# First weights and samples asked for by counts and the eight largest of one row; the first pair as a plain product

## The chip, the cores and the metric

The kernel runs on one core of a Trainium2 chip. The metric is device time in microseconds (us), from runs of the whole program; beside them stands one profiled execution, from which every view of the profile comes.

## What is computed

There are 128 samples of 128 tokens with 1024 features, and an integer role (one of three) for each sample. Two layers follow each other, and in both the sample's role picks the weights, the biases and the vectors of the normalisation:

```python
h = jnp.einsum('bsh,bhk->bsk', hidden_states, W_down[role]) + b_down[role][:, None, :]   # 1024 -> 512
h = jax.nn.gelu(h, approximate=False)
u = jnp.einsum('bsk,bkh->bsh', h, W_up[role]) + b_up[role][:, None, :]                   # 512 -> 1024
y = hidden_states + u
mean = jnp.mean(y, axis=-1, keepdims=True)
var = jnp.mean(jnp.square(y - mean), axis=-1, keepdims=True)
yn = (y - mean) * jax.lax.rsqrt(var + LN_EPS)
return yn * gamma[role][:, None, :] + beta[role][:, None, :]
```

All of it is in float32. The roles are known only on the chip.

## The kernel before, in words

**Order of the samples.** Because weights depend on the role, the kernel first sorts the samples by role, on the chip. The roles come in one DMA as a row of 128 integers (L249). VectorE cleans the row (L282 to L284), TensorE turns it into a column, comparisons and two matmuls count roles and ranks (L290 to L300), and a few dozen small VectorE operations give each sample its slot. The role with the most samples gets place 0, and so on. Three matmuls in `gathered` (L323 to L330) make three small integer rows: `perm` (which sample stands in slot n, L332), `role_of` (which role has place k, L343) and `place` (which place slot n has, L348). An engine that issues a DMA for "the sample of slot 0" or "the weights of place 0" first loads such a number into a register (`reg`, L351), so it waits for the row it reads. `counted` (L241) is a VectorE operation with a sum along the row; `zeros` (L264) issues matmuls of 128x512 zeros whose results nobody reads; nine of them stand behind the sort (L349).

**Pairs.** Two samples of one role make a pair (256 tokens). There are 63 such pairs and one last item for samples left over. Four phases follow each other (down and up of the first layer, down and up of the second), and each goes over all items. In a down phase a pair is multiplied with a 1024x512 weight by a seven-product scheme of the Strassen-Winograd kind (`item_products`, L431): the two samples are the two halves of the rows, the features and the columns are halved too, and seven products of 128x256 blocks, with four steps over the features each, take the place of eight. For this the weights must be given as blocks and differences of blocks (B11, B21, B22, T1, T2, T3, T4; for the first phase `first_sum`, L159, makes the T blocks out of the raw rows), and three sums of the pair's own blocks are needed (`winograd_sums`, L396). The bias gets in by a copy of the bias table into the accumulator bank ahead of the products (`seeded`, L424), where the right half of the table holds right minus left (`subtract`).

**A down item.** `load` and `load_rest` fetch the two samples in four quarters each, by SP's queue (`quartered`, L382). `turn` (L526) transposes a sample in 32x32 blocks on VectorE; `prepare` (L536) turns both samples and makes the sums (on GpSimd, for the first pair on VectorE), and for the first pair it makes T1 as well. Then the seven products follow, and the results go through a Gelu on ScalarE into the tensor `hd` in memory.

**Order of the work.** Every step is put on a heap with a time in units of a product slot (seven to a pair, 1.727 us each) and taken off in order of time (`at`, L734, and the loop at the end). On each engine the instructions are chained in that order, DMA requests on the queues of SP and ACT included. So each queue is strictly in order, and an instruction that waits holds up all that is behind it on its own engine. The first pair has times of its own (L474), with the product of T1 second.

**First weights.** The raw rows of place 0 (1024x512, 2 MB) are fetched in two blocks of 1 MB, `rows_of[0]` and `rows_of[1]`. `load_rows` (L145) makes four requests for a block, one for each quarter of the partitions, and the block's requests are split over the queues of ACT and SP; the second ACT half of block 1 stands behind the first two seeds on ACT. All of them read `role_of`, and the samples' requests read `perm`.

Of the kernel before, what the change touches and what calls it, by code (L numbers as in the profile page):

```python
# [26 lines left out]
def kernel(  # L27
# [117 lines left out]
    def load_rows(k, place, engine, kind, quadrants=range(NQ)):  # L145
        w = layers[0][0]
        role = reg(role_of, place, [kind], R - 1)
        for q in quadrants:
            src = w[ds(role, 1), ds(q * H // NQ, H // NQ), :]
            src = src.rearrange("o (i m) c -> i (o m) c", i=SQ)  # L150
            engine.dma_start(
                rows_of[k][ts(q, SQ), place].rearrange("p j h c -> p j (h c)"), src[:, ts(k, NQ)]
            )
# [87 lines left out]
    def counted(o, in0, scalar, op0, in1):  # L241

        n = in0.shape[1]
        nc.vector.scalar_tensor_tensor(
            junk[:, 0:n], in0, scalar, in1, op0, ALU.mult, accum_out=o
        )
# [22 lines left out]
    iota_row, iota_col, ones, upper = f32(B), f32(1), f32(B), f32(B)  # L269
    junk, wide = f32(B), f32(SQ)  # L270
    iota_r, ones_r = iota_row[:, 0:R], ones[:, 0:R]
    eps = const.tile([P, 1], F32, name="eps")
    nc.vector.memset(eps, LN_EPS)
    nc.vector.memset(ones, 1.0)
    nc.vector.tensor_copy(iota_row, iota_i)
    nc.vector.tensor_copy(iota_col, iota_c)
    nc.vector.tensor_scalar(upper, iota_row, iota_col, None, ALU.is_gt)
    nc.vector.tensor_copy(wide, iota_col.to_broadcast((P, SQ)))


    role_row = f32(B)[0:1]
    nc.vector.tensor_scalar(role_row, raw, float(-R), float(R - 1), ALU.max, ALU.min)  # L282
    nc.vector.tensor_scalar(junk[0:1], role_row, 0.0, float(R), ALU.is_lt, ALU.mult)
    nc.vector.tensor_tensor(role_row, role_row, junk[0:1], ALU.add)  # L284
# [4 lines left out]
    ps = bank_a("own_ps")  # L289
    nc.tensor.matmul(ps[:, 0:1], role_row, ones[0:1, 0:1], start=True, stop=True)  # L290
    role_col, is_own = f32(1), f32(R)
    nc.vector.tensor_copy(role_col, ps[:, 0:1])
    nc.vector.tensor_scalar(is_own, iota_r, role_col, None, ALU.is_equal)

    ps = bank_a("count_ps")
    nc.tensor.matmul(ps[:, 0:R], upper, is_own, start=True, stop=True)
    nc.tensor.matmul(ps[:, R : 2 * R], ones, is_own, start=True, stop=True)
    counts = f32(2 * R)
    nc.vector.tensor_copy(counts, ps[:, 0 : 2 * R])
    before, count = counts[:, 0:R], counts[:, R : 2 * R]  # L300

    key, odd, even = f32(R), f32(R), f32(R)
    nc.vector.scalar_tensor_tensor(key, count, float(R + 1), iota_r, ALU.mult, ALU.subtract)
    count_i = const.tile([P, R], I32, name="count_i")
    nc.vector.tensor_copy(count_i, count)
    nc.vector.tensor_scalar(count_i, count_i, 1, None, ALU.bitwise_and)
    nc.vector.tensor_copy(odd, count_i)
    nc.vector.tensor_tensor(even, count, odd, ALU.subtract)

    rank, own_key, base_, rest, own, slot, left, move = (f32(1) for _ in range(8))  # L310
    counted(own_key, is_own, 1.0, ALU.mult, key)
    counted(rank, is_own, 1.0, ALU.mult, before)
    counted(own, is_own, 1.0, ALU.mult, even)
    counted(base_, key, own_key, ALU.is_gt, even)
    counted(rest, key, own_key, ALU.is_gt, odd)
    nc.vector.tensor_tensor(slot, base_, rank, ALU.add)
    nc.vector.tensor_tensor(left, rank, own, ALU.is_ge)
# [3 lines left out]
    nc.vector.tensor_scalar(onehot, iota_row, slot, None, ALU.is_equal)  # L321

# [9 lines left out]
    perm = gathered("perm", wide, onehot)  # L332

# [9 lines left out]
    role_of = gathered("role_of", wide[0:R], at_place)  # L343

# [4 lines left out]
    zeros("bbbeeebbb")  # L349
# [32 lines left out]
    def quartered(t, srcs):  # L382

        for s, src in enumerate(srcs):
            n = src.shape[-1] // NQ
            for q in range(NQ):
                nc.sync.dma_start(
                    t[s][ts(q, SQ)], src[:, ts(q, n)].rearrange("(a t) c -> t a c", t=SQ)
                )
# [41 lines left out]
    def item_products(item, cols):  # L431
# [9 lines left out]
        if n < NPAIR:  # L441
            r = item.places[0]

            def s1():
                product(ps["b"], A(0, 0), w["B11"], r, cols)
                item.begin(0, 0, ps["b"])

            def s2():
                ps["a"] = bank("a", item.tag)
                product(ps["a"], A(0, 1), w["B21"], r, cols, True)  # L450
                item.end(0, 0, ps["a"])

            def s3():
                product(ps["b"], sums[:, 0], w["T2"], r, cols)
                item.begin(0, 1, ps["b"])

            def s4():
                product(ps["e"], A(1, 0), w["T1"], r, cols)
                item.begin(1, 1, ps["e"])

            def s5():
                product(ps["b"], sums[:, 1], w["T3"], r, cols)
                item.end(1, 1, ps["b"])

            def s6():
                product(ps["e"], sums[:, 2], w["B22"], r, cols)
                item.end(0, 1, ps["e"])

            def s7():
                product(ps["b"], A(1, 1), w["T4"], r, cols)  # L470
                item.whole(1, 0, ps["b"])


            times = (0, 2, 4, 1, 6.5, 6, 8) if item.early else range(0, 14, 2)  # L474
            steps = list(zip(times, (s1, s2, s3, s4, s5, s6, s7)))
            te = -3.9 if item.early else 1.5
            return steps + [(item.SEED, lambda: seed("b", "b", r)), (te, lambda: seed("e", "e", r))]
# [25 lines left out]
    class Down:  # L503
# [7 lines left out]
        def load(self):  # L511
            if self.among_weights:


                block = self.ph.weights[ORDER[self.m]].v
                self.xq = [block[:, 1 + s] for s in range(2)]
            else:
                self.xq = [flat("q", 4, f"xq{self.tag}_{s}", H) for s in range(2)]
            self.xq = [t.rearrange("p (a c) -> p a c", a=NQ) for t in self.xq]
            self.srcs = x_of(self.layer, self.n, ENG.SP)  # L520
            quartered(self.xq[0:1], self.srcs[0:1])

        def load_rest(self):
            quartered(self.xq[1:2], self.srcs[1:2])

        def turn(self, s):  # L526
            nc.vector.transpose(  # L527
                self.a[:, s].rearrange("p j (t a) -> p j a t", t=SQ),
                self.xq[s].rearrange("p a (i j) -> p j a i", i=SQ),
            )  # L530

        def begin_turns(self):
            self.a = flat("t", 3, "xT" + self.tag).rearrange("p (s j c) -> p s j c", s=2, c=P)
            self.turn(0)

        def prepare(self):  # L536
            if not self.among_weights:
                self.begin_turns()
            if self.early:
                first_sum("T1", 0)  # L540
            self.turn(1)
            self.sums = None
            if self.n < NPAIR:
                self.sums = flat("s", 3, "S" + self.tag, 1792)[:, 0:1536].rearrange(
                    "p (m j c) -> p m j c", m=3, c=P
                )
                winograd_sums(self.sums, self.a, nc.vector if self.early else nc.gpsimd)
            set_places(self, [ENG.PE, ENG.Activation])

        def products(self):  # L550
            return [(-0.5, self.first)] + item_products(self, K // 2)
# [191 lines left out]
    for k, ph in enumerate(phases):  # L743
        for m, n in enumerate(sequence):
# [17 lines left out]
            elif k == 0:  # L762
                first = {0: -30, 1: -19, 2: -19, 3: -17.4}.get(m, -19)
                rest = -27 if m == 0 else first + 0.05
            else:
                first = -15 if m == 0 else -11.9
                rest = first + 0.1
# [10 lines left out]
            prepare = {1: 3.5 - base, 2: 8.6 - base}.get(m, kind.PREPARE) if k == 0 else kind.PREPARE  # L778
# [4 lines left out]
        if k + 1 < len(phases):  # L783
# [17 lines left out]
            else:  # L801


                def first_bias(nxt=nxt):
                    nxt.bias = row = const.tile([P, 1, K], F32, name="first_bias")
# [45 lines left out]
    at(-29, lambda: load_bias([0], nc.scalar))  # L851
    at(-29, lambda: load_rows(0, 0, nc.scalar, ENG.Activation, (0, 1)))
    at(-28, lambda: load_rows(0, 0, nc.sync, ENG.SP, (2, 3)))
    at(-27, lambda: subtract(slice(0, 1)))
    at(-26, lambda: load_rows(1, 0, nc.sync, ENG.SP, (2, 3)))
    at(-3, lambda: load_rows(1, 0, nc.scalar, ENG.Activation, (0, 1)))
    for i, name in enumerate(("T2", "T3", "T4")):
        at(-2.5 + i / 10, lambda name=name: first_sum(name, 0))
    at(14.7, lambda: load_bias(range(1, R)))
    at(20.7, lambda: subtract(slice(1, R)))  # L860
    for k in range(1, R):
        start = SLOTS * 2 * k
        at(start + 4.25, lambda k=k: load_rows(0, k, nc.sync, ENG.SP))
        at(start + 8.25, lambda k=k: load_rows(1, k, nc.sync, ENG.SP))
# [44 lines left out]
```

## Time and profile before

| what | value |
|---|---|
| median of 3 runs | 3143.81 us (3142.12 to 3145.17) |
| profiled execution | 3143.59 us |
| its span, first to last instruction | 3141.8 us |
| TensorE busy | 3109.3 us, 99% of the span |
| VectorE, ScalarE, GpSimd busy | 1977.3, 1203.6, 1793.9 us |
| `perm` ready, `role_of` ready | 9.06, 10.45 us after the span's start |
| first matmul of the first pair | 20.85 us |
| first matmul of the second pair | 39.72 us |
| DMA over the span | 642.21 MB, 204 GB/s |

Times in the views are microseconds from the span's start. PE is TensorE, PEld its weight loads, DVE is VectorE, ACT ScalarE, POOL GpSimd, SP the engine that issues most DMAs; a "q" behind a name is the engine's queue of instructions that aren't counted as busy. A name such as `xTd<-xqd` says what is written and what is read; "[4.78 <-DVE xTd L402]" is idle time of the engine ahead of the instruction and what ended it. A float32 matmul is two instructions in the trace.

### The profile page before, as it was taken

The page shows a single profiled execution, that of the slowest core. Times are in us where ns is not written, and L with a number is a line of the kernel's source. Part 1 is how long each engine was busy: PE and PEld are TensorE (multiplying, and loading weights), DVE is VectorE, ACT ScalarE, POOL GpSimd, SP SyncE. Part 2 cuts the span into 40 slices and gives each one's busy share as a digit, 9 for nine tenths or more (in the row PEclk, how much of TensorE's full clock was granted, in tenths as well). Part 3 has the DMA queues.
Part 4 walks back from the last instruction along what each step waited for, and adds up shares of the span by engine and source line. Part 5 has one row for each costly group of instructions (what it writes and reads, how often), then busy time and mean ns, then how long its engine had stood idle before and what let it go on. Part 6 is the DMA issues. An engine that isn't in the chain of part 4 may idle for free.

```text
span 3141.8 us, 42319 instructions
## 1 busy us (share of the span) xinstructions
PE 3109.3 (99%) x10806; PEld 2053.3 (65%) x10806; DVE 1977.3 (63%) x2794; ACT 1203.6 (38%) x2814; POOL 1793.9 (57%) x1396
## 2 busy tenths in 40 slices
PE   8999999999999999999999999999999999999998
PEld 6888888888544444444478888888884444444443
DVE  5655445454578777788854444444447777787777
ACT  1222222222445455555432222222224545554554
POOL 3544444444577767777654443444436777677776
PEclk9999999999999999999999999999999999999999
DMA  8888878886786666666796555555568766666665
GB/s 191 207 209 213 209 206 210 212 213 191 278 286 222 218 217 218 217 223 216 235 260 164 128 135 128 134 125 137 126 184 292 264 219 216 218 217 221 215 226 175
DMA packets 430165, 642.21 MB, mean 204 GB/s; under 512 B 36081, under 2 KB 305906, under 8 KB 428786
## 3 DMA queue, kind: packets, MB, share of 16 engines
q1 hardware_dynamic: 429458, 637.94, 69.1%
q8 instruction: 102, 1.67, 0.2%
q10 hardware_dynamic: 480, 1.57, 0.2%
q14 instruction: 125, 1.02, 0.1%
HBM read 405.01 MB, written 234.36 MB: 204 GB/s over the span
## 4 chain that ended last, share of the span: by engine, by line
PE 48%; DMA 1%; DVE 1%; issue 0%; ACT 0%; DVEq 0%; SPq 0%; ACTq 0%
PE bu L410 14%; PE bd L410 14%; PE eu L410 7%; PE ed L410 7%; PE au L410 3%; PE ad L410 3%; DMA mid<-ou 0%; DVE ou L719 0%; DMA wall<-mid 0%; DMA hd<-hd 0%; ACT ou L704 0%; DVE xu L635 0%; DVE last_stat L636 0%; DVE xu L638 0%; DVEq L905 0%
## 5 line engine op out<-in xcount | busy, mean ns | idle before, releaser
L410 PE MATMUL bu<-wall,hTu 128*128 (+1 forms) x2048 | 922.0, 592 | 2.1 <-POOL ou L717 0.7
L527 DVE STREAM_TRANSPOSE xTd<-xqd 128x1024 f32<-128x1024 f32 x250 | 505.0, 2087 | 354.1 <-PE bd L410 275.4
L410 PEld LDWEIGHTS bu<-wall,hTu 128*128 128x128 f32 x2048 | 388.7, 190 | 490.9 <-issue 455.6
L401 POOL TENSOR_TENSOR Sd<-xTd 128x512 f32<-128x512 f32 x125 | 160.5, 1284 | 802.6 <-DVE xTd L527 798.7
L706 POOL TENSOR_TENSOR varu<-varu,mhalf 128x1 f32<-128x1 f32 x254 | 333.7, 1314 | 383.1 <-ACT varu L705 383.1
L410 PE MATMUL bd<-wall,xTd 128*128 (+1 forms) x2080 | 490.9, 379 | 1.4 <-DMA wall<-T 0.8
L410 PE MATMUL eu<-wall,hTu 128*128 (+1 forms) x1040 | 488.0, 592 | 0.0
L709 DVE SCALAR_TENSOR_TENSOR ou<-xu,meanu,tables 128x1024 f32<-128x1024 f32 x254 | 327.1, 1288 | 253.3 <-ACT ou L704 253.0
L410 PE MATMUL bd<-wall,Sd 128*128 (+1 forms) x2016 | 476.5, 379 | 2.3 <-ACT hd L560 1.6
L410 PEld LDWEIGHTS bd<-wall,xTd 128*128 128x128 f32 x2080 | 394.9, 190 | 58.0 <-issue 3.5
L410 PEld LDWEIGHTS bd<-wall,Sd 128*128 128x128 f32 x2016 | 382.8, 190 | 56.7 <-issue 4.1
L565 ACT ACTIVATE hd<-hd 128x256 f32<-128x256 f32 x382 | 159.4, 418 | 536.4 <-DVE hd L564 536.4
L410 PEld LDWEIGHTS eu<-wall,hTu 128*128 128x128 f32 x1040 | 197.6, 190 | 247.5 <-issue 229.6
L700 ACT ACTIVATE partu<-statu 128x2 f32<-128x2 f32 x254 | 51.9, 204 | 730.6 <-DVE xu L638 730.6
L717 POOL TENSOR_TENSOR ou<-ou,tables 128x1024 f32<-128x1024 f32 x127 | 299.5, 2358 | 0.1
L704 ACT ACTIVATE ou<-xu,meanu 128x1024 f32<-128x1024 f32 x254 | 292.2, 1150 | 8.3
L410 PE MATMUL ed<-wall,xTd 128*128 (+1 forms) x1072 | 254.6, 381 | 4.8 <-DVE xTd L402 4.8
L401 POOL TENSOR_TENSOR hTu<-hTu 128x256 f32<-128x256 f32 x126 | 205.3, 1630 | 66.3 <-DVE hTu L607 54.4
L410 PE MATMUL ed<-wall,Sd 128*128 (+1 forms) x1008 | 238.2, 379 | 0.1
L410 PE MATMUL ad<-wall,xTd 128*128 (+1 forms) x1008 | 238.2, 379 | 0.0
L410 PE MATMUL au<-wall,hTu 128*128 (+1 forms) x504 | 236.8, 592 | 0.0
L410 PEld LDWEIGHTS ed<-wall,xTd 128*128 128x128 f32 x1072 | 204.5, 191 | 33.6 <-issue 5.6
(114 smaller groups left out, 3349.8 us busy)
## 6 DMA issues: line engine op xcount, KB each, us to landing
xqd<-in_x_dram SPq DMA_DIRECT2D x512, 128.0 KB, 3.3
hd<-hd SPq DMA_DIRECT2D x256, 256.0 KB, 2.4
xu<-in_x_dram SPq DMA_DIRECT2D x128, 512.0 KB, 5.0
mid<-ou SPq DMA_DIRECT2D x128, 512.0 KB, 6.1
xu<-mid SPq DMA_DIRECT2D x128, 512.0 KB, 5.8
out_dram<-ou SPq DMA_DIRECT2D x126, 512.0 KB, 5.5
hqu<-hd SPq DMA_DIRECT2D x244, 256.0 KB, 6.5
xqd<-mid SPq DMA_DIRECT2D x488, 128.0 KB, 3.8
```

What stands on the lines that cost most here:

```text
L401: engine.tensor_tensor(dst[:, 1], a11, a21, ALU.subtract)
L410: nc.tensor.matmul(ps[:, 0:cols], a[:, j], w.rhs(r, j, cols), start=start and j == 0, stop=j == n - 1, skip_group_check=True,)
L527: nc.vector.transpose(self.a[:, s].rearrange("p j (t a) -> p j a t", t=SQ), self.xq[s].rearrange("p a (i j) -> p j a i", i=SQ),)
L565: nc.scalar.activation(y, y, AF.Gelu)
L700: nc.scalar.mul(part, self.stat[:, s], -1.0 / H)
L704: nc.scalar.activation(box["o"], self.x[:, s], AF.Square, bias=m, accum_out=v)
L706: nc.gpsimd.tensor_tensor(v, v, mhalf[:, 0:1], ALU.pow)
L709: nc.vector.scalar_tensor_tensor(box["o"], self.x[:, s], box["m"][:, 0:1], row(self.ph.gamma), ALU.add, ALU.mult)
L717: nc.gpsimd.tensor_tensor(o, o, row(self.ph.beta), ALU.add)
```

## The change

Five things are changed together.

1. The roles are counted on one row of one partition, by three `counted` operations; the role with the largest key comes out as an integer `role_0`, and the first samples of that role come out by the operation that gives the eight largest of a row (`first_two`, of which two are used). Both stand ahead of the sort. A matmul copies the row with roles, counts and keys to all partitions, and the sort goes on from there with three 128-wide counts. Zero matmuls are spread over the sort instead of standing behind it.
2. The first pair's samples, the weights' rows of place 0 and the first bias row are asked for by `role_0` and `first_two`. A block of rows is one request of 128 partitions (for all places). Block 0 is asked for on ACT, block 1 on SP; the first sample's quarters are split over SP and ACT.
3. The first pair doesn't use the seven products: `plain` multiplies each sample with the raw rows, in 512 columns, behind a one-row matmul that puts in the bias. Its samples are turned in halves. It makes no sums.
4. T1 to T4 of place 0 are made at new times; the bias table's first row is loaded later on ACT (-26 instead of -29), and its difference is taken at 0.3.
5. The second pair (m = 1) keeps the default order of products, its `prepare` goes from 3.5 to 4.5, and its sums are made on VectorE.

```diff
-    def load_rows(k, place, engine, kind, quadrants=range(NQ)):
-        w = layers[0][0]
-        role = reg(role_of, place, [kind], R - 1)
-        for q in quadrants:
-            src = w[ds(role, 1), ds(q * H // NQ, H // NQ), :]
-            src = src.rearrange("o (i m) c -> i (o m) c", i=SQ)
-            engine.dma_start(
-                rows_of[k][ts(q, SQ), place].rearrange("p j h c -> p j (h c)"), src[:, ts(k, NQ)]
-            )
+    def load_rows(k, place, queue):
+        role = reg(role_of, place, [queue.engine], R - 1) if place else reg(role_0, 0, [queue.engine], R - 1)
+        src = layers[0][0][ds(role, 1)].rearrange("o (p m) c -> p (o m) c", p=P)
+        queue.dma_start(rows_of[k][:, place].rearrange("p j h c -> p j (h c)"), src[:, ts(k, NQ)])
...
+    zeros("bb")
...
+    nc.vector.tensor_scalar(falling, iota_row[0:1], -1.0, float(B), ALU.mult, ALU.add)
+    nc.vector.tensor_scalar(same, iota_row, iota_col, None, ALU.is_equal)
+    nc.vector.tensor_scalar(earlier, iota_row, iota_col, None, ALU.is_lt)
+    row = f32(B + 2 * R)
+    role_1, count_1, key_1 = row[0:1, 0:B], row[0:1, B : B + R], row[0:1, B + R :]
...
+    for r in range(R):
+        counted(count_1[:, r : r + 1], role_1, float(r), ALU.is_equal, ones[0:1])
+    nc.vector.scalar_tensor_tensor(key_1, count_1, float(R + 1), iota_r[0:1], ALU.mult, ALU.subtract)
+    ps = bank_a("row_ps")
+    nc.tensor.matmul(ps[:, 0 : B + 2 * R], ones[0:1, 0:P], row[0:1], start=True, stop=True)
+    zeros("beee")
+    role_row, key = ps[:, 0:B], f32(R)
...
+    nc.vector.tensor_reduce(top, key_1, AX.X, ALU.max)
+    counted(role_f, key_1, top, ALU.is_equal, iota_r[0:1])
+    role_0 = const.tile([1, 1], I32, name="role_0")
+    nc.vector.tensor_copy(role_0, role_f)
+    nc.vector.scalar_tensor_tensor(junk[0:1], role_1, role_f, falling, ALU.is_equal, ALU.mult)
+    nc.vector.max(out=first_f, in_=junk[0:1])
+    first_two = const.tile([1, 8], I32, name="first_two")
+    nc.vector.tensor_scalar(first_two, first_f, -1.0, float(B), ALU.mult, ALU.add)
+    nc.vector.tensor_copy(counts[:, 0:R], ps[:, B : B + R])
+    nc.vector.tensor_copy(key, ps[:, B + R : B + 2 * R])
+    counted(role_col, role_row, 1.0, ALU.mult, same)
+    counted(rank, role_row, role_col, ALU.is_equal, earlier)
+    counted(counts[:, R:], role_row, role_col, ALU.is_equal, ones)
...
     perm = gathered("perm", wide, onehot)
+    zeros("bb")
...
     role_of = gathered("role_of", wide[0:R], at_place)
+    zeros("bb")
...
     place = gathered("place", wide_place, onehot)
-    zeros("bbbeeebbb")
+    zeros("bb")
...
+            if self.early:
+                for k, queue in enumerate((nc.sync, nc.scalar)):
+                    quartered(self.xq[0:1], [self.early_x(0, queue.engine)], (2 * k, 2 * k + 1), queue)
+                return
...
+    def plain(self):
+        self.ps = [None, None]
+        def half(s, k):
+            if k == 0:
+                self.ps[s] = bank("a", f"{self.tag}_{s}")
+                nc.tensor.matmul(self.ps[s], ones[0:1, 0:P], bias_row, start=True, stop=False)
+            for j in range(NQ):
+                rows = rows_of[k][:, 0, j].rearrange("p h c -> p (h c)")
+                nc.tensor.matmul(
+                    self.ps[s], self.a[:, s, NQ * k + j], rows, start=False, stop=k == 1 and j == NQ - 1
+                )
+            if k == 1:
+                nc.scalar.activation(self.h[s], self.ps[s], AF.Gelu)
+        steps = [(4 * s + 2 * k, lambda s=s, k=k: half(s, k)) for s in range(2) for k in range(2)]
+        return steps + [(0.1 + k / 10, lambda k=k: self.turn(1, ts(k, NQ))) for k in range(2)]
...
-            prepare = {1: 3.5 - base, 2: 8.6 - base}.get(m, kind.PREPARE) if k == 0 else kind.PREPARE
+            prepare = {1: 4.5 - base, 2: 8.6 - base}.get(m, kind.PREPARE) if k == 0 else kind.PREPARE
...
-    at(-29, lambda: load_bias([0], nc.scalar))
-    at(-29, lambda: load_rows(0, 0, nc.scalar, ENG.Activation, (0, 1)))
-    at(-28, lambda: load_rows(0, 0, nc.sync, ENG.SP, (2, 3)))
-    at(-27, lambda: subtract(slice(0, 1)))
-    at(-26, lambda: load_rows(1, 0, nc.sync, ENG.SP, (2, 3)))
-    at(-3, lambda: load_rows(1, 0, nc.scalar, ENG.Activation, (0, 1)))
-    for i, name in enumerate(("T2", "T3", "T4")):
-        at(-2.5 + i / 10, lambda name=name: first_sum(name, 0))
+    at(-31, lambda: load_rows(0, 0, nc.scalar))
+    at(-30.5, load_bias_row)
+    at(-29, lambda: load_rows(1, 0, nc.sync))
+    at(-26, lambda: load_bias([0], nc.scalar))
+    at(0.3, lambda: subtract(slice(0, 1)))
+    for t, name in zip((-8.7, -2.5, 4.6, 4.7), ("T1", "T2", "T3", "T4")):
+        at(t, lambda name=name: first_sum(name, 0))
```

The first bias row shares one small tile (`first_rows`) with the first bias of layer 1, which had a tile of its own. `load_bias_row` is a DMA of one row on ACT. The first sample is asked for at -30, the second at -28 (it was -27).

## The prediction

> **What bounds the kernel now.** I read the page first, then the busy time in stretches, then the start-up instruction by instruction, then the DMA queues. The page:
>
> ```profile
> span 3141.8 us, 42319 instructions
> PE 3109.3 (99%) x10806; PEld 2053.3 (65%) x10806; DVE 1977.3 (63%) x2794; ACT 1203.6 (38%) x2814; POOL 1793.9 (57%) x1396
> ```
>
> TensorE is busy all but 32.5 us. Stretches (length, then busy time of each engine, granted clock, DMA share, GB/s):
>
> ```profile
> 0.00:21.00 21.00, 12.43 (x31) 5.98 (x32) 9.56 (x48) 2.17 (x4) 1.10 (x7) 1.00 0.43 107
> 21.00:27.60 6.60, 1.82 (x9) 1.29 (x9) 4.36 (x5) 0.37 (x1) 0.00 (x0) 1.00 0.98 227
> 27.60:39.72 12.12, 12.12 (x48) 10.38 (x49) 11.23 (x10) 2.27 (x6) 4.28 (x3) 0.86 0.91 192
> 39.72:51.81 12.09, 12.09 (x58) 10.64 (x57) 7.74 (x6) 3.53 (x10) 11.54 (x10) 1.00 0.91 231
> ```
>
> The second pair starts at 39.72 and from there a pair costs 12.09 us without a gap (7 products of 1.727). So what matters is when TensorE may begin the second pair; after that everything follows it. The start-up, from the timeline (start, length, engine, line):
>
> ```profile
> 2.17 0.21 DVE L282 TENSOR_SCALAR sorting<-raw 1x128 f32<-1x128 int32 x1
> ...
> 8.78 0.28 DVE L329 CAST perm<-perm_ps 1x128 int32<-1x128 f32 x1 [0.73 <-PE perm_ps L327]
> ...
> 10.09 1.92 SPq L387 DMA_DIRECT2D xqd<-in_x_dram  x4
> 10.30 0.15 DVE L329 CAST role_of<-role_of_ps 1x3 int32<-1x3 f32 x1 [0.42 <-PE role_of_ps L327]
> ...
> 12.09 0.86 ACTq L151 DMA_DIRECT2D wall<-in_L_cond_W_down_dram  x2
> ...
> 20.85 1.97 PE L410 MATMUL bd<-wall,xTd 128*128 128x256 f32 x8
> ...
> 27.60 3.58 PE L410 MATMUL ed<-wall,xTd 128*128 128x256 f32 x8 [4.78 <-DVE xTd L402]
> ```
>
> Samples are asked for 7.9 us after the roles are read (2.17 to 10.09), weights 9.9 us after. One product runs at 20.85, then TensorE waits 4.78 us for the second sample and its sums, and restarts at a low clock. The transfers between 13 and 15 us, by queue (q1 is SP, q10 ACT; packets, MB, share):
>
> ```profile
> q10 hardware_dynamic: 135, 0.39, 82.4%
> q1 hardware_dynamic: 146, 0.15, 23.7%
> ```
>
> While both queues run, weights (ACT) take 195 GB/s and samples (SP) 73, together 266. One more line, from SP's own waits:
>
> ```profile
> SPq L151 <- DMA tables<-in_L_cond_b_down_dram: 2.6, 1, 2.6
> ```
>
> SP's second weight request, at 15.64, waits for the bias DMA, eight requests earlier: the waits fit eight completion semaphores used in turn.
>
> [...] weight loads of the zero matmuls stand 0.86 us apart at 12.50 and 13.36, and 0.43 from 14.18. [...]
>
> **The change, part by part.**
>
> *Count and first eight on one row.* Two mask rows more stand ahead of the roles (about 0.5 us), so the clean row of roles, done at 2.94 now, is done at 3.4. Three counts: a 3-wide count has a cadence of 0.21 to 0.27, and 128 elements cost 0.13 more (L277 0.29 against L303 0.16), so 0.35 each: 4.45. Key, largest, role and integer copy: 0.2 + 0.2 + 0.35 + 0.2. The role is ready at 5.4 instead of 10.45. First samples: 0.3 for the marked row, the largest-eight between 0.2 (nearest row) and 0.8, I take 0.35, and 0.2: 6.2 instead of 9.06. The tensor reduction isn't in the trace either: 0.15 to 0.4.
>
> *Requests.* From role to ACT's first request now: 10.45 to 11.15, 0.7; a further register load brings the next 0.94 later. So block 0 of weights is asked for at 6.1 on ACT, the bias row (2 KB) at 7.0, the sample quarters 2 and 3 at 8.0 and 8.5. SP, with two register loads as now (9.06 to 10.09): quarters 0 and 1 at 7.2 and 7.7, block 1 at 8.6, then sample 1. Its second quarter waits for block 0, eight requests earlier.
>
> *Transfers.* Data flows 0.9 us after a request (asked 10.09, first bytes at 11.0). Block 0 (1.05 MB) has 0.26 MB by 8.0, then 195 GB/s beside the samples' 73: quarters 0 and 1 (0.26 MB) are through at 11.6, block 0 near 12.0. Quarters 2 and 3 stand behind it on ACT's ring and meet block 1 on SP's: 0.26 MB at 73 is 3.6 us, 15.6[...]. The bounds: only block 0 ahead (1.57 MB at 266 from 7.0) gives 13.4, everything but sample 1 ahead (2.6 MB) 17.3. Block 1 lands near 17.5, sample 1 near 20.5.
>
> *Turning* is cut in halves of 1.05 (2.09 now for 128x1024): first half of sample 0 at 17.2, second at 18.2.
>
> *Sort and zero matmuls.* The rest of the sort now follows: two copies, three 128-wide counts (0.4 each) and the old steps. From the counts' copy (5.14) to the one-hot's end (8.04) took 2.9; plus 1.2 and 0.4 for the copies and the shifted masks, less 0.63 for the three small counts that go: 3.9. From 6.2: 10.1, and with the moved `wide` and `eps` the permutation's matmul goes at 10.3 instead of 8.11. Then in TensorE's order: 0.65, two zeros (4 x 0.43 = 1.71), roles 0.25, 1.71, places 0.6, 1.71: 16.95. The first bias matmul (512 columns, 2 x 0.43 = 0.86) needs no sample: 17.8. DVE's steps between (0.9 to 1.3) hide under the zeros. So TensorE's own queue ends 0.6 after the first half turn, and sets the start: **17.8**, clock open.
>
> *Plain product.* 16 matmuls of 512 columns at 0.855 are 13.7, and the second bias matmul 0.86: 14.55. The first pair ends at **32.4**. The seven products would be 12.09, so this form costs 3.3 with both bias matmuls, one of them hidden, but needs no sums and no differences of weights. Its later needs: block 1 at 21.2 (landed 17.5), sample 1 turned at 25.5: DVE does T1 (1.22) to 19.4, T2 to 20.6, both half turns to 22.7.
>
> *The second pair, m = 1,* takes over the early sums. DVE: bias differences to 23.2, its two turns to 27.4 (its samples, asked for between 16 and 21 as semaphores come free, land by 25), three sums of 0.69 to 29.8, T3, which overwrites block 0 and so waits for the third half product (28.9), to 31, T4 to 32.3. First product 32.4 needs B11 and its first turn (25.3); T2 at 35.9, T3 at 39.3. Cover 4 us or more; cost zero, and one for one once it is gone.
>
> *Moved.* The bias table's load now waits on ACT for the sorted role (13.2). Behind it on ACT stands the first Gelu, at 24.7: eleven us of cover. On SP nothing that pair 0 needs stands behind a sorted value; pair 1's samples need the permutation (11.3) and are held by semaphores until 16 anyway. Later rows of weights are one request instead of four (four take 1.85 to 2.26 us of SP now): same bytes, same ring, and TensorE waits for none of them: zero. The bias row of layer 1 shares a tile long free: zero.
>
> *Sum.* 39.72 − 32.4 = **7.3 us** earlier, and the stream behind is unchanged: 3141.8 − 7.3 = 3134.5 span. The profiled execution took 3143.59, 1.79 around its span: 3136.3. The median of the runs is 0.22 above it: **3136.5**.
>
> **Rivals.** About 0.2% (6.3 us) is what measurement tells from no change here.
> - *Start by TensorE's queue*, as above: gain 6.3 to 9.5 (DVE's unknown operations move it by under 1 us). For: sample 0 has 0.6 us to spare. Chance 0.60.
> - *Transfers set the start.* The sample's second half is on the ring behind 1 MB and beside another MB. If it lands at 19.1 (2.6 MB ahead, at 225 GB/s), the product starts at 20.2, gain 5.0: 3138.8. Against: the early slices moved 265 to 280. Gain 3.5 to 6.3; chance 0.26.
> - *Pair 1 isn't ready.* Its samples and sums, T3 behind the third half product: a slip beyond the 4 us cover eats the gain, 1 to 3.5 left, about 3141. Chance 0.09. With it I count that the role doesn't come out much before the sort.
> - *Slower: block 1 late.* It shares with quarters 2 and 3, then the bias table, and all of the second half products need it. After it lands, 3.43 + 0.86 + 6.85 = 11.1 us follow, so from a landing at 28.6 on the pair ends later than now. Today its last quarter lands at 27.9 (asked for only at 23.45). At 30 the kernel would be 1.4 slower: 3145.2. Against: it is asked for at 8.6 and waits for no semaphore. Chance 0.05, of which 0.02 by over 0.2%.
>
> **Numbers.** Faster by over 0.2%: 0.60 (first case). Within: 0.26 + 0.09 + 0.03 = 0.38. Slower: 0.02. The range takes the first two cases whole, gain 9.5 to 3.5 us: 3134.3 to 3140.3; 0.14 is left out, and the median's own scatter (about 1 us) takes some more.
>
> **What would show it.** Role as integer near 5.4, weights' request near 6.1; sample 0's last quarter landed 15 to 17; first plain matmul near 17.8, straight after a bias matmul; halves of 3.43; pair 1's first product at 32.4 without a wait, and 12.09 per pair from there. A wait of the first plain matmul for DVE's turn or a DMA says the second case; a gap ahead of pair 1's products the third; one ahead of the second half product the fourth. [...]

## The result, and the profile after

The changed kernel takes 3139.8 us (median of 19 runs, 3137.38 to 3141.12) against 3144.54 us for the kernel before, in 19 runs: a ratio of 0.9985, 95% interval 0.9979 to 0.9991. That is 4.7 us less, 0.15%, where 7.3 us had been forecast. The profiled execution took 3138.75 us, its span is 3137.0.

The page of the changed kernel, span and busy times:

```profile
span 3137.0 us, 42212 instructions
PE 3116.2 (99%) x10788; PEld 2050.2 (65%) x10788; DVE 1978.0 (63%) x2808; ACT 1199.6 (38%) x2807; POOL 1787.2 (57%) x1392
```

TensorE's idle time fell from 32.5 to 20.8 us, by 11.7, while its busy time rose by 6.9: the difference is the 4.8 us of the span. The same stretches as before, cut where the first pair now ends (length, busy time by engine, granted clock, DMA share, GB/s):

```profile
0.00:21.00 21.00, 19.21 (x37) 7.35 (x38) 12.87 (x64) 1.49 (x2) 1.09 (x7) 1.00 0.70 188
21.00:34.80 13.80, 13.80 (x33) 5.72 (x32) 12.48 (x12) 0.87 (x2) 1.26 (x1) 1.00 0.73 190
34.80:46.89 12.09, 12.09 (x58) 10.64 (x57) 7.95 (x6) 3.75 (x10) 8.54 (x7) 1.00 0.68 177
```

From 34.80 on seven products again take 12.09 us without a gap. The start-up, from the timeline (PEld lines are the weight loads of single passes; a float32 matmul is two passes in these traces, as the permutation's x2 shows):

```profile
4.78 0.14 DVE L300 CAST role<-sorting 1x1 int32<-1x1 f32 x1
5.22 0.28 DVE L302 MAX8 sorting<-sorting 1x8 f32<-1x128 f32 x1
5.63 0.40 ACTq L148 DMA_DIRECT2D wall<-in_L_cond_W_down_dram  x1
7.77 0.84 ACTq L402 DMA_DIRECT2D xqd<-in_x_dram  x2
8.11 4.05 PE L262 MATMUL e_zero<-sorting 128*128 128x512 f32 x6
9.55 0.29 DVE L328 TENSOR_SCALAR sorting<-sorting 128x128 f32<-128x128 f32 x1
9.82 0.34 PEld L262 LDWEIGHTS e_zero<-sorting 128*128 128x128 f32 x1 [0.52 <-issue]
10.67 0.23 PEld L262 LDWEIGHTS e_zero<-sorting 128*128 128x128 f32 x1 [0.52 <-issue]
11.15 0.19 PEld L262 LDWEIGHTS e_zero<-sorting 128*128 128x128 f32 x1 [0.24 <-issue]
12.10 0.41 PE L336 MATMUL perm_ps<-sorting 128*32 128x128 f32 x2
17.46 2.12 DVE L547 STREAM_TRANSPOSE xTd<-xqd 128x512 f32<-128x512 f32 x2 [0.33 <-DMA xqd<-in_x_dram]
18.66 1.12 PE L582 MATMUL ad<-first_rows,sorting 1*128 1x512 f32 x2
19.71 7.13 PE L585 MATMUL ad<-wall,xTd 128*128 128x512 f32 x16
26.77 1.12 PE L582 MATMUL ad<-first_rows,sorting 1*128 1x512 f32 x2
27.83 7.13 PE L585 MATMUL ad<-wall,xTd 128*128 128x512 f32 x16
36.52 1.89 PE L425 MATMUL ad<-wall,xTd 128*128 128x256 f32 x8
```

The weights are asked for at 5.63 instead of 12.09. The one-hot row of the sort is ready at 9.84, but the matmul that uses it, the permutation's, runs at 12.10. Six zero passes stand ahead of it (8.11, 4.05 us), and the first of them run at the low clock. From 12.10 on the queue goes as forecast, only later.

"Low clock" means here that the passes of 512 columns stand 0.85 us apart (9.82 to 10.67) instead of 0.43 (12.97 to 13.40). The column of granted clock doesn't show it in the start-up: it reads 1.00 from 0 to 21 us, because the record of the clock that the trace keeps begins only with the moment at which the clock opens, 10.75 us here. Later stretches at half the clock do show in the column (0.50 from 27.79 to 31.21 in the kernel before). (The 592 ns of two expectations below is how long the profile draws one pass at the full clock, not the distance between passes.)

The mark used below for the lead is the second pair's product with B21, its second: at 41.45 before, at 36.52 after, so 4.93 earlier. By then the same products are done in both. The line of the kernel before, to be set against the last one above:

```profile
41.45 1.89 PE L410 MATMUL ad<-wall,xTd 128*128 128x256 f32 x8
```

(In the kernel before, the second pair's first product ran at 37.99, ahead of the first pair's last, so the 39.72 of the table and the prediction is the moment at which seven products were done, not the first matmul of the second pair. The count is the same.) The first up product comes at 797.73 before and at 792.80 after: the lead is carried unchanged.

### The profile page after: what moved, and what is told of

Read it like the earlier page. It is cut to its first block, busy times and chain, and to the rows that moved or that the text cites. A ratio compares the mean times of both kernels' runs of the same rounds, so it can differ in the third digit from the quotient of the medians.

```text
span 3137.0 us, 42212 instructions
## 1 busy us (share of the span) xinstructions
PE 3116.2 (99%) x10788; PEld 2050.2 (65%) x10788; DVE 1978.0 (63%) x2808; ACT 1199.6 (38%) x2807; POOL 1787.2 (57%) x1392
## 5 line engine op out<-in xcount | busy, mean ns | idle before, releaser
L547 DVE STREAM_TRANSPOSE xTd<-xqd 128x1024 f32<-128x1024 f32 (+1 forms) x252 | 505.8, 2071 | 351.0 <-PE bd L425 262.2
L425 PEld LDWEIGHTS ed<-wall,xTd 128*128 128x128 f32 x1064 | 202.2, 190 | 27.9 <-issue 0.5
```

Of the source, the lines that this page charges most:

```text
L425: nc.tensor.matmul(ps[:, 0:cols], a[:, j], w.rhs(r, j, cols), start=start and j == 0, stop=j == n - 1, skip_group_check=True,)
L547: nc.vector.transpose(self.a[:, s, chunks].rearrange("p j (t a) -> p j a t", t=SQ), self.xq[s].rearrange("p a (i j) -> p j a i", i=SQ)[:, ...
```

## The experiments

All change the changed kernel. The columns: the moment at which the trace's record has the clock open, the permutation's matmul, the first matmul on the first pair's samples, the second pair's B21 product (all us from the start of the trace), the span, the median time, and its ratio with the interval to runs of the kernel before on the same chip (their medians go from 3143.86 to 3144.61). All but the time and the ratio come from one profile each.

| kernel | clock opens | perm | first | B21 | span | time | ratio |
|---|---|---|---|---|---|---|---|
| before | 14.14 | 8.11 | 20.85 | 41.45 | 3141.8 | 3144.54 | |
| after | 10.75 | 12.10 | 19.71 | 36.52 | 3137.0 | 3139.8 | 0.9985 (0.9979 to 0.9991) |
| after, again | 11.32 | 12.38 | 19.99 | 36.81 | 3139.2 | 3141.0 (one run) | |
| after, third | 6.15 | 9.96 | 18.27 | 35.08 | 3135.7 | 3139.99 | 0.9986 (0.9980 to 0.9993) |
| late asks | 5.04 | 9.46 | 24.24 | 43.37 | 3143.3 | 3148.48 | 1.0014 (1.0007 to 1.0021) |
| seven products | 11.09 | 12.27 | 21.17 | 37.90 | 3139.2 | 3141.8 | 0.9994 (0.9985 to 1.0002) |
| no last zeros | 6.28 | 9.99 | 18.35 | 35.16 | 3136.2 | 3139.43 | 0.9985 (0.9978 to 0.9991) |
| six zeros | 10.96 | 12.20 | 18.11 | 36.44 | 3138.1 | 3140.66 | 0.9991 (0.9982 to 1.0000) |
| biases first | 11.29 | 12.37 | 18.93 | 34.49 | 3135.5 | 3138.06 | 0.9980 (0.9973 to 0.9986) |
| sample first | 5.02 | 9.45 | 19.75 | 39.38 | 3141.2 | 3142.11 | 0.9993 (0.9984 to 1.0002) |
| sample on SP | 5.36 | 9.62 | 16.18 | 31.74 | 3134.7 | 3137.04 | 0.9979 (0.9969 to 0.9988) |
| spread zeros | 13.96 | 9.98 | 17.75 | 34.80 | 3135.7 | 3137.64 | 0.9980 (0.9972 to 0.9988) |
| places later | 4.78 | 9.33 | 15.07 | 32.82 | 3133.6 | 3135.79 | 0.9975 (0.9965 to 0.9986) |

**Late asks.**

```diff
-role = ... if place else reg(role_0, 0, [queue.engine], R - 1)
+role = ... if place else reg(role_of, 0, [queue.engine], R - 1)
-x[ds(reg(first_two, s, [engine], B - 1), 1)]
+x[ds(reg(perm, s, [engine], B - 1), 1)]
```

(and `role_of` for the bias row.)

> The changed kernel, but the weights, bias row and samples of place 0 are asked for by the sorted rows again (role_of, perm); plain product, zeros and the one-row counts stay. Theory (the early requests are the whole gain, the plain product gives none): ACT's first request moves from 5.6 to about 15.3 us, the first sample's last quarter lands about 9 us later, the first plain matmul moves from 19.7 to about 28, the first pair ends near 43 instead of 34.8, span 3144 to 3147, slower than the kernel before by 2 to 5 us. Rival (the plain product is worth several us by itself): no slower than the kernel before, span 3141 or less.

The kernel is slower than the one before, by 4.4 us in the runs. In the trace the B21 product stands at 43.37, 1.92 later than before and 6.85 later than after. So the early requests are the whole gain. Of the 6.85, 4.53 are the later start (24.24 against 19.71) and 2.3 a first half at the low clock (0.51 granted between 24 and 29 us), behind waits of 4.31 and 1.77 us. The requests went out earlier than I had said (12.8, not 15.3), because the clock opened early in this trace and the roles' gather came at 11.7. When it opens late, as in the trace of after, the roles are ready 2.6 us later (14.75 against 12.12); that could be the rest of the loss in the runs, but it is argued, not traced. Timeline of this run:

```profile
13.74 0.51 ACTq L898 DMA_DIRECT2D first_rows<-in_L_cond_b_down_dram  x1
20.41 2.07 PE L582 MATMUL ad<-first_rows,sorting 1*128 1x512 f32 x2 [4.31 <-DMA first_rows<-in_L_cond_b_down_dram]
24.24 1.22 PE L585 MATMUL ad<-wall,xTd 128*128 128x512 f32 x1 [1.77 <-DVE xTd L547]
```

The bias row, 2 KB, took 6.7 us to come: it stands behind 1 MB of weights on ACT's ring. In the changed kernel it has time until 18.66.

**Seven products.**

```diff
-self.plain() if self.early else item_products(self, K // 2)
+item_products(self, K // 2)
```

(with the first pair's times, turns, sums and differences of the kernel before, and the bias table asked for by `role_0`.)

> The changed kernel, with its early requests (the bias table too by role_0), counts and zeros, but the first pair by the seven products in the order of the kernel before, whole turns, early sums for the first pair. Theory (products save 3.3 us of TensorE's time but wait for differences and sums on VectorE, so the two forms cost about the same): TensorE's first product near 20, a wait of 3 to 5 us after it, span within 1.5 us of the changed kernel's 3137.0. Rival (the plain form is what saves time, since nothing waits for VectorE): span 3140 or more.

Measured between the two: span 3139.2, time 3141.8. From the first product to the B21 product it takes 16.73 us, against 16.81 for the plain form. So the two forms do cost the same here, as the theory had it, but not in its way: the wait behind the first product is 0.97 us, not 3 to 5, and about 1.7 us go to the low clock, which this trace has from 21.33 to 24.75, after a wait for the sample (the product at 21.17 takes 3.60 us, the next 1.97). The 1.4 us by which it comes later lie ahead of the first product (21.17 against 19.71): there it waits for a whole turn instead of a half, and that turn begins only at 19.01, on VectorE behind the difference of the bias table, which had waited for the table until 18.67.

**No last zeros, six zeros.**

```diff
     place = gathered("place", wide_place, onehot)
-    zeros("bb")
```

(six zeros: the two pairs behind `perm` and `role_of` go as well.)

> The changed kernel without the two zero matmuls behind the third gather. Theory (TensorE's own queue sets the start; the turned half of the first sample has been ready since 18.5): the first plain matmul goes from 19.7 to about 18.6, span down by about 1.1 to 3135.9, clock still open. Rival (the sample's transfer sets the start): first plain matmul stays at 19.7, span 3137.0.

First plain matmul at 18.35, near the forecast but by another cause, and span 0.8 less. This trace has the permutation's matmul at 9.99, not at 12.10, with nothing changed ahead of it: the clock had opened 4.5 us earlier (6.28, not 10.75). Here it is the sample that sets the start: TensorE waited 2.60 us for the turn, and the turn 2.15 for the DMA. The time, 3139.43, isn't to be told from the changed kernel's.

> The changed kernel without the six zero matmuls behind the three gathers; the six ahead of them, which the accumulator banks need, stay. Theory (the zeros behind the gathers pay for themselves by the clock): first plain matmul near 18.6, but at the low clock, 592 ns and more of pitch per pass for 3 to 6 us, so 1.5 to 3 us lost against the run without the last two alone; span 3136.5 to 3139. Rival (the clock stays open over a gap of about 3 us, the zeros only cost): span 3135.9 or less.

The start came to 18.11, and the first eight matmuls took longer. The line of this run, to be set against "19.71 7.13" above:

```profile
18.11 8.65 PE L582 MATMUL ad<-wall,xTd 128*128 128x512 f32 x16 [1.90 <-DVE xTd L544]
```

1.5 us are lost to the low clock: the passes stand 0.85 us apart (19.13 to 19.98) and 0.43 from 21.45 on. That refutes the rival's open clock. The zeros behind the gathers pay for about what they cost: the median is 1.2 us above that of no last zeros, with intervals that overlap.

**Again, and a third time.** The unaltered kernel, for the moment at which the clock opens.

> The changed kernel once more, unaltered, for the moment at which the clock opens: it opened at 10.8 us in its profile, near 7.2 in that of the run without the last zeros and at 14.2 in that of the kernel before[...]. Theory (that moment is chance, and decides when TensorE reaches the permutation's matmul): another opening moment is possible; if it is near 7, the permutation's matmul stands near 10.0 instead of 12.1 and the first plain matmul near 18.4 (by the sample) instead of 19.7, span about 1.3 less; if it is near 11 again, nothing moves. Rival (the opening moment is set by the program): 10.8 and 19.7 again.

> The changed kernel unaltered, on the same chip and against the same runs of the kernel before, for the size of the lead and one more opening moment of the clock. First plain matmul 19.7 to 20.0 if the clock opens near 11, near 18.4 if near 7; time 3.5 to 6 us less than the kernel before, and 2 to 5 more than the run with the places later.

(The "near 7.2" in the first of these is 1 us off: the records have the clock open at 6.28 without the last zeros and at 6.15 in the third profile.) Again: zeros of 4.33 us, first plain matmul at 19.99. The third:

```profile
6.76 0.19 PEld L262 LDWEIGHTS e_zero<-sorting 128*128 128x128 f32 x1 [0.24 <-issue]
7.19 2.74 PE L262 MATMUL e_zero<-sorting 128*128 128x512 f32 x6
9.96 0.41 PE L336 MATMUL perm_ps<-sorting 128*32 128x128 f32 x2
14.72 0.28 DVE L338 CAST place<-place_ps 1x128 int32<-1x128 f32 x1 [1.75 <-PE place_ps L336]
16.53 1.12 PE L582 MATMUL ad<-first_rows,sorting 1*128 1x512 f32 x2
17.09 2.13 DVE L547 STREAM_TRANSPOSE xTd<-xqd 128x512 f32<-128x512 f32 x2 [2.09 <-DMA xqd<-in_x_dram]
18.27 7.13 PE L585 MATMUL ad<-wall,xTd 128*128 128x512 f32 x16 [0.62 <-DVE xTd L547]
```

The same six passes take 2.74 us instead of 4.05. The same program reaches the permutation's matmul 2.1 us earlier and would be through its queue at 17.6; then the sample, landed near 17, is what it waits for. So the moment isn't set by the program (10.75, 11.32 and 6.15 us), and there are two bounds close together: the queue at 17.6 to 20.0, the sample at 18.3. In 21 runs beside the third profile the changed kernel took 3139.99 us, 4.4 less than the kernel before; the profiled execution itself, 3137.50, was the lowest of them.

**Both biases first.**

```diff
-                if k == 0:
-                    self.ps[s] = bank("a", f"{self.tag}_{s}")
...
+                if k == 0 and s == 0:
+                    for i in range(2):
+                        self.ps[i] = bank("a", f"{self.tag}_{i}")
...
```

(The bias matmul follows its bank in both forms. The last zeros are left out here too.)

> The run without the last zeros, with both bias matmuls ahead of the first half product, where TensorE waited 2.6 us for the turned sample. Theory (the second bias matmul, 1.05 us with its change of operand, lies on the path between the halves, the first does not): first plain matmul stays near 18.3, the second pair comes 1.0 earlier, span 3135.2. Rival (the half products wait for block 1 or the second sample's turn there anyway): no change, 3136.2.

Span 3135.5, time 3138.06. From the first plain matmul to the second pair's first product are now 13.84 us (18.93 to 32.77), where it had been 15.09 with the second bias matmul between. So against the run without the last zeros B21 comes 0.67 earlier (34.49 against 35.16), though the clock opened late in this trace and the start is 0.58 later (18.93 against 18.35).

**Sample first, sample on SP.**

```diff
 sample first:
-    at(-31, lambda: load_rows(0, 0, nc.scalar))
-    at(-30.5, load_bias_row)
+    at(-31, load_bias_row)
+    at(-29.5, lambda: load_rows(0, 0, nc.scalar))
 sample on SP (on top of both biases first):
-for k, queue in enumerate((nc.sync, nc.scalar)):
-    quartered(self.xq[0:1], [self.early_x(0, queue.engine)], (2 * k, 2 * k + 1), queue)
+quartered(self.xq[0:1], [self.early_x(0, ENG.SP)])
```

> The run without the last zeros, where ACT asks for the bias row and the first sample's last two quarters before block 0 of the weights. Theory (sample packets of 1 KB get almost nothing while weight packets of 8 KB are on the other ring, 0.01 of 0.77 MB between 8 and 10 us, so the last quarter landed at 17): the sample lands near 10 to 12, block 0 near 14, and TensorE's queue sets the start again, near 15.8; second pair 2.5 earlier, span 3133.5 to 3134.5. Rival (total bytes decide, and weights that come later cost what the sample gains): start not before 17.5, span 3135.5 or more.

My theory failed here. The sample did come early, and block 0 came late. Timeline and, from the transfers between 10 and 12 us, the only queue with data:

```profile
14.81 2.12 DVE L546 STREAM_TRANSPOSE xTd<-xqd 128x512 f32<-128x512 f32 x2 [0.33 <-issue]
19.75 4.60 PE L584 MATMUL ad<-wall,xTd 128*128 128x512 f32 x5 [4.53 <-DMA wall<-in_L_cond_W_down_dram]
```

```profile
q1 hardware_dynamic: 74, 0.61, 89.3%
```

SP's block 1, asked for 0.5 us ahead of ACT's block 0, took all of the transfer in these 2 us, though it is needed second. From 12 to 16 us both rings moved, packet for packet (121 of ACT against 132 of SP, which also carried samples), and ACT's ring had 0.97 of 1.33 MB; both blocks landed near 19.5. TensorE waited 4.53 us, and then ran at the low clock (passes 0.86 us apart, 20.73 to 21.59). In the next run what comes second stands behind what comes first on the same ring.

> The run with both biases first and without the last zeros, where all four quarters of the first sample are asked for on SP, ahead of block 1, and ACT keeps block 0 as its first request. Theory (block 0 goes first at some 380 GB/s, then the sample meets no weights, since block 1 stands behind it on the same ring): sample landed near 13 instead of 17.4, block 0 near 11.5, block 1 near 17; TensorE's queue alone sets the start, near 16.5 if the clock opens near 7 and near 19 if it opens near 11; span 3133 to 3135.7. Rival (block 1, pushed back, is late for the second half product): a gap ahead of that, span above 3136.

That is what this run does: start at 16.18, as forecast, B21 at 31.74, span 3134.7, time 3137.04. From the timeline:

```profile
13.93 0.41 PE L336 MATMUL place_ps<-sorting 128*32 128x128 f32 x2
14.97 2.13 DVE L545 STREAM_TRANSPOSE xTd<-xqd 128x512 f32<-128x512 f32 x2 [0.32 <-issue]
16.18 4.13 PE L584 MATMUL ad<-wall,xTd 128*128 128x512 f32 x9
```

The turn now waits for no data, yet begins only behind the third gather. On VectorE the copy of the places stands ahead of the turn, and it waits for TensorE. But of 9.7 us of lead over the kernel before at B21 only 7.1 are left in the span: nearly all of the rest goes at the border of the two layers, where TensorE waited 2.16 us for ScalarE's copy of `hd` until 1598.45 and had half the clock for 3.41 us from 1599.39 on (0.57 granted between 1599 and 1603), which alone is 1.7 us. The early start is in part the early clock of this trace (5.36, against 11.29 in biases first, which places the permutation's matmul 2.75 later, as much as B21). The ratios of the two, 0.9979 and 0.9980, can't be told apart: that the sample on SP gains over biases first isn't shown in the time.

**Spread zeros** (on top of the sample on SP).

```diff
-    zeros("beee")     # row
+    zeros("b")
-    zeros("bb")       # perm
+    zeros("ee")
-    zeros("bb")       # role_of
+    zeros("e")
```

> As the run with the sample on SP, with only the six zero matmuls that the banks need, three ahead of the permutation's matmul, two behind it and one behind the roles'. Theory (zeros at the low clock ahead of the permutation's matmul were the term missed, 1.8 us): that matmul stands near 10.0 whenever the clock opens, the queue is through near 16.5, start 16 to 17, span 3133 to 3135. Rival (with less work between, the clock is closed at the start and half of 4 to 6 us is lost): start near 16, but the first halves at 592 ns and more per pass for some us, span 3135.5 or more.

The permutation's matmul stands at 9.98 although the clock was closed: the zero passes behind it stand 0.85 us apart. That is the missed term shown by itself. But the clock opened only at 13.96 and was at half again from 17.37 to 20.79, so the start came to 17.75, and from there to the second pair's first product are 15.3 us instead of 13.84. Against biases first, whose clock opened late too, the start is 1.18 earlier and B21 0.31 later: what the zeros had cost ahead of the permutation was given back. Span 3135.7 is the rival's.

**Places later** (on top of the sample on SP).

```diff
-    role_of = gathered(...); zeros("bb")
-    own_place ...; place = gathered("place", wide_place, onehot)
+    role_of = gathered(...)
+    at(-8.6, begin_place); at(6.2, end_place)
```

> The run with the sample on SP and both biases first, where the third gather (places, first needed by pair 21) moves behind the first pair and the two zeros behind the roles' gather go. In all runs so far the first sample's turn began 0.32 to 0.33 us after the copy of the places, unless the sample itself was late: VectorE's queue held it behind the third gather. Theory: the turn begins with the sample, near 12.7, or 0.33 after the copy of the roles, whichever is later; first plain matmul 2.2 earlier than with the sample on SP, near 14 if the clock opens near 7 and near 17 if it opens near 11; span 2 less for the same moment of opening, 3132 to 3135. Rival (the layers' boundary, where the run with the sample on SP lost 2.5 us of its lead, gives the rest back too): start near 14, but span 3134.5 or more.

The turn began at 13.89, when the sample had landed, and the start came to 15.07. The sample came 1 us later than I had put it, and TensorE's wait of 1.37 us ended with the clock at half (15.02 to 18.44). Busy time and clock (0.63) from 14 us on:

```profile
14.00:18.00 4.00, 2.93 (x4) 1.37 (x5) 3.97 (x7) 0.00 (x0) 0.00 (x0) 0.63 1.04 287
18.00:22.00 4.00, 4.00 (x10) 1.67 (x10) 2.48 (x3) 0.00 (x0) 0.00 (x0) 0.95 0.84 189
```

So B21 stands at 32.82, 1.1 later than with the sample on SP, while the median of 3135.79 is the lowest of all: 0.9975 (0.9965 to 0.9986) of the kernel before, whose interval overlaps the sample on SP's. It beats the kernel before and the changed kernel (3139.99 on the same chip); that it beats the sample on SP isn't shown.

## Why the prediction was right and wrong

**The bound** was right: the end follows the moment at which TensorE starts on the second pair's products. The lead of 4.93 us at 36.52 is 4.93 at the first up product and 4.8 in the span; from B21 to the first up product it is 756.28 us in both kernels.

**The range** held, in part by luck. The measured gain of 4.7 us lies below the 6.3 to 9.5 of the first case, whose mechanism (TensorE's own queue sets the start) is what the profile on record shows. It lies in the 3.5 to 6.3 of the second case, whose mechanism isn't at work there. A cost that neither case named brought it there.

**Counts, first samples, requests** came a little earlier than worked out. Role as integer 4.92 (5.4), the largest eight 0.28 us (0.35), reduction 0.14 (0.15 to 0.4), first request 5.63 (6.1), last quarters 7.77 and 8.28 (8.0 and 8.5).

**Transfers.** The shares were wrong, and so was the reading under them: of ACT's 135 packets between 13 and 15 us in the kernel before, 96 were the bias table's of 2 KB and only 23 were weights, of 8 KB. So the 195 GB/s were no rate of weights. Between 8 and 10 us in the changed kernel, by queue (packets, MB, share):

```profile
q10 hardware_dynamic: 98, 0.76, 92.0%
q1 hardware_dynamic: 7, 0.01, 1.0%
```

I had taken 195 GB/s for weights and 73 for samples. It was 380 and 5. By packets the two queues were near even in the kernel before (146 against 135) but not in these 2 us, with 98 against 7: the samples were asked for 0.8 us and more after block 0, and got next to nothing until its last packet was through, at 10.64 instead of 12; why is not shown. After that block 1 held back quarters 2 and 3, this time near even by packets, 73 against 71 between 12 and 14 us, which with 8 KB against 1 KB is 0.60 of 0.66 MB. The sample landed at 16.97. The forecast's 17.2 for its first turned half, less 1.05, had put that near 16.1, with an estimate of the author's for the time from the last packet to the landing, which is 0.93 here (16.04 to 16.97). The landing is within the stated bounds of 13.4 to 17.3: a block 0 that was early and quarters that were slow nearly cancelled.

**Sort and zero matmuls: the step that failed.** "Then in TensorE's order: 0.65, two zeros" began at 10.3, and the start at 17.8 had "clock open". VectorE was ready at 9.92, ahead of the forecast. But the four zeros behind the row were priced at no cost. With most of them at the low clock, 0.85 us apart, they last until 12.0, so the permutation's matmul is 1.8 late; from it to the first plain matmul are 7.6 us, where 7.5 were worked out. In the third profile, with the clock open at 6.15, the same step ends near 17.6. So the mechanism was right, and the cost of the zeros ahead of the permutation's matmul was put at nothing, which holds only if the clock is open early. Eleven traces have the same zeros up to that matmul (all but the kernel before and spread zeros): six have the clock open between 4.78 and 6.28 us, five between 10.75 and 11.32. That the clock would be open ahead of the permutation's matmul was the author's assumption: it fits the six, not the five. What part of the 2.6 us missing in the medians is the clock isn't shown: a median may mix executions of both kinds.

**Plain product.** 15.09 from first matmul to end, where 14.55 had been worked out. The 16 matmuls go at the forecast pace. The second bias matmul between them costs 1.25 us instead of 0.86, as biases first shows by taking it out (15.09 against 13.84), and some 0.1 goes where the second pair's products follow. That is 0.5 us.

**The sum.** 7.3 less 1.9 for the start (1.8 of it the zeros), less 0.5 for the plain product, is 4.9, which is the lead measured. In the third profile the lead is 6.37, and the 0.9 missing are about 0.5 of later start, by the sample, and about 0.5 of plain product.

**The rivals.** "Transfers set the start" is true in the third profile and without the last zeros (start 18.3), not in the one on record; its figure of 5.0 us came about all the same, by another cause. "Pair 1 isn't ready" is refuted: TensorE waits for nothing between 19.71 and 46.9. "Block 1 late" is refuted for the changed kernel, where block 1 landed at 16.15; sample first shows the mechanism, in block 0. (Before, its last quarter landed at 27.45, not at 27.9.)

**What stays open.** The time at the border of the layers varies by about 2 us between profiles of the same program: from the first up product to the first down product of layer 1 it is 772.17 us in the profile on record, 774.32 again, 772.92 in the third, 772.46 before. So a single span doesn't tell gains of 1 or 2 us apart. In sample on SP 1.7 of the 2.5 us lost there are the stretch at half the clock; the changed kernel has such a stretch too, of 3.41 us from 1574.05 on, and the kernel before has none there. Why TensorE waits longer at the border in some profiles isn't settled.

## What to carry to other kernels

The zero passes ran 0.85 us apart until the clock was open, and 0.43 from then on, and the opening came at 4.78 us in one trace and at 11.32 in another. So price such work at the low pace where it stands ahead of a matmul on the critical chain. Moving it behind that matmul frees the matmul (9.98 instead of 12.10 in spread zeros), but there the clock opened later (13.96) and the gain was given back (B21 at 34.80, against 34.49 in biases first), so both sides have to be priced. Requests that are needed first should be first on a ring of their own, and what is needed second should stand behind them on the same ring: two rings at once didn't share by need in these runs (0.61 MB for block 1 and nothing for block 0 between 10 and 12 us in sample first, start at 19.75; 16.18 in sample on SP). And when a start is brought forward, list all that stands in order ahead of it on each engine, copies for later use too: here the turn waited for the third gather, which nobody needs for twenty pairs.

## What was not expected of the hardware

- The same program's clock opened at 6.15 us in one profile and at 10.75 and 11.32 in two others. The stretches that follow in the records of the clock are close to 3.41 us or whole multiples of it: 13.65 open and 3.41 at half in the kernel before (from 14.14 and 27.79), 10.24 open and 3.42 at half in places later (from 4.78 and 15.02), 3.41 open and 3.42 at half in spread zeros (from 13.96 and 17.37). What sets the first moment isn't shown.
- How long TensorE waits doesn't alone tell whether the clock falls: a wait of 2.60 us left it open in no last zeros, one of 1.37 us in places later came with 3.41 us at half.
- With 8 KB weight packets on one ring and 1 KB sample packets on the other, the samples got 0.01 of 0.77 MB in 2 us, where 2 KB and 8 KB packets together in the kernel before had left them 0.15 of 0.54. In sample first, one ring of 8 KB packets got nothing for 2 us beside another that had begun earlier, and the larger part in the 4 us behind them (0.97 of 1.33 MB).
- A 1 MB request moved at 380 GB/s (0.76 MB in 2 us) while the other ring got next to nothing, more than the mix in the start-up of the kernel before (292 GB/s between 12 and 14 us, 266 between 13 and 15).
